# Masked attention layer on one core: where the late tiles are turned, which engine forms two block sums, and when one bias row is subtracted

## The chip, the cores and the metric

The kernel runs on one core of a Trainium2 chip. The metric is the device time of one execution in microseconds (us). The engines are named as the profile names them: PE is TensorE, DVE is VectorE, ACT is ScalarE, POOL is GpSimd, SP is SyncE; PEld is PE's weight load.

## What is computed

The input x has 2708 rows of 1024 numbers, adj is a 2708 x 2708 matrix of zeros and ones with about four ones in a row. In float32:

```python
h = relu(layernorm(x))
q, k, v = h @ Wq.T + bq, h @ Wk.T + bk, h @ Wv.T + bv
z = (q @ k.T) / 32 * adj
z = where(z == 0, -10000, z)
out = x + relu(softmax(z, axis=1) @ v)
```

## The kernel before

**The algebra.** Because a row of adj has few ones, nothing of size 2708 x 2708 is multiplied. Three products of matrices are left: M = Wq.T Wk, made once; "q" rows h M; and the output rows u Wv.T, where u is the weighted sum of those rows of h that the ones of adj name. A score is the dot product of one q row with one row of h, and both scores and weighted sums are made row by row on DVE, from rows of h that POOL gathers out of DRAM (`gather`, L611).

**Tiles and units.** Rows are sorted by their number of ones and cut into tiles of 128. The main loop (from L1244) goes over *units*. A unit is a pair of tiles that is multiplied by a 1024 x 1024 matrix with seven block products instead of eight, as Strassen and Winograd do it. Units 0 to 9 are "q" pairs, units 10 to 19 are "o" (output) pairs, and one single tile comes last. The attention of all tiles is a generator (`attention`), of which `advance(us)` takes as many steps as fit into the time given; a step of a score or of a sum counts as 1.3.

**One unit on PE.** `multiply` runs the blocks in the order s2, a12, s4, s3, then a11 and s1 *of the next unit* (`opened`), then its own a22. A block is four matmul instructions of 128x512, 8 records in the trace. Between blocks it calls `after(i)`, where everything else is issued: after(0) and after(1) stand ahead of s2, after(2) behind s2, after(3) behind a12, after(4) behind s4, after(5) behind s3 and after(6) at the end. DVE's order is that of the program text (`manual_schedule`); the orders of ACT, POOL, SP and PE in the late units are a scheduler's.

**Turning a pair.** The tiles must stand with columns in partitions. `blocks` (L712 on) returns `upper`, called in after(0) of the unit before, and `lower`, called in after(2). There are two ways:
- *by PE*: eight 128x128 transposes of a tile into PSUM (L416), which ACT copies out for a11, a12 and a22 (L719), while DVE makes s1 and s3 out of PSUM (L723);
- *faced*: ACT rewrites the finished u row into v with its columns rearranged (L962) and stores it (`u_dram`, L964); SP loads it back in four pieces of 32 rows (`by_quarters`, L701); DVE transposes 32x32 squares (`faces`, L706), one instruction for each of the two halves of a tile, and then forms s1 (L723) and s3 (L743).

The sums s2 = s1 - a11 and s4 = a12 - s2 (L723) are made by DVE or by POOL, as the caller of `blocks` says: by POOL for units 1 and 2 and for every pair with a faced tile, otherwise by DVE.

**Which tiles are faced** is decided at the end of `sums` (L957 to L968). A tile that is done more than about two units before its own unit is faced, except the last single one; a tile done later is `held` in SBUF when its unit is near, or else stored unturned by SP (L968) and loaded back in one piece (L1226).

**The end of a block product.** In an o unit, c12 (after block s4) is a DVE sum (L1144) and a ReLU on ACT (L1145); c22 (after s3) is a copy out of PSUM on ACT, `taken` (L1094), a DVE sum (L1140) and a ReLU (L1141). PE's block a22 writes the bank that `taken` has read, so it waits for it. In q units the same places are L1113 and L1110.

**The bias row.** `bp_sb` holds the row that starts the PSUM banks of a pair (`banks_for`, L761). It is q's bias until unit 9's banks are filled; at after(4) of unit 8 SP loads b_v into it (L1327) and DVE subtracts one half from the other (L1328).

**Pace.** `share` (L1252) is what `advance` gets at each of a unit's seven calls: 20/7 in q units, 19/7 in o units, less 0.75/7 for each faced tile of the next pair.

Of the kernel before, what the change touches and what calls it, by code (L numbers as in the profile page):

```python
# [65 lines left out]
def tile_preln_masked_attention(  # L66
# [12 lines left out]
    nc = tc.nc  # L79
# [97 lines left out]
    t = 0  # L177
    while t < NT:
# [4 lines left out]
        t = e  # L183
# [28 lines left out]
    def row_tile(name):  # L212
        return work.tile([P, D], FT, tag="row", name=name, bufs=ROWS)
# [401 lines left out]
    rows_of = {}  # L615
    FIRST = EARLY // 2
# [92 lines left out]
    def is_faced(xt):  # L709
        return any(xt is y for y in faced)  # L710
# [57 lines left out]
    ops_of = {0: blocks(*rows_of.pop(0))}  # L768
# [88 lines left out]
    def fill():  # L857
        while wanted and free:
            t, s = wanted.pop(0)
            g = free.pop(0)  # L860
            if s == K[t]:
                half = slice(HOSTS.index(t) * HP, (HOSTS.index(t) + 1) * HP)
                nc.gpsimd.dma_start(g[:HP], v_dram[half, :])
            else:
                with tc.issue_after(first_q[0].ins) if first_q else nullcontext():
                    gathered.append(gather(g, h_dram[:, :], t, s, P, skip=True))
            g_of[t].append(g)

    def chained(step):

        with tc.issue_after(chain[-1].ins):
            chain.append(step())
# [64 lines left out]
    def sums(t):  # L937
        u, coef, m = us.pop(t)
        for s in range(0 if t in EMPTY else 1, K[t]):
            fill()  # L940
            chained(lambda: nc.vector.scalar_tensor_tensor(  # L941
                u, g_of[t][s], coef[:, s:s + 1], u, op0=ALU.mult, op1=ALU.add))
            free.append(g_of[t][s])
            yield 1.3
        fill()
        if t in HOSTS:
            chained(lambda: nc.vector.scalar_tensor_tensor(
                u[:HP], g_of[t][K[t]][:HP], m[:HP, 3:4], u[:HP], op0=ALU.mult, op1=ALU.add))
            free.append(g_of[t][K[t]])
            yield 1.3  # L950
            fill()
        g_of.pop(t)
        if t == SECOND:
            nc.sync.dma_start(v_dram, u)
            whole_second.append(True)
            return
        unit = next((n for n, pair in enumerate(units) if pair[0] == "o" and t in pair[1:]), len(units))  # L957
        if now < [unit - 2, 2] and t != alone:
            faced_tiles.add(t)
        if t in faced_tiles:  # L960
            v = row_tile(f"v_{t}")
            nc.scalar.copy(v.rearrange("p (a c r) -> p c a r", a=QUADS, r=QP),  # L962
                           u.rearrange("p (c a r) -> p c a r", a=QUADS, r=QP))
            nc.scalar.dma_start(u_dram[t * P:(t + 1) * P, :], v)  # L964
        elif near(t):
            held[t] = u
        else:
            nc.sync.dma_start(u_dram[t * P:(t + 1) * P, :], u)  # L968
        done.add(t)
# [37 lines left out]
    faced_tiles, whole_second = set(), []  # L1007
# [4 lines left out]
    spent, now = [0.0], [0, 0]  # L1012
# [193 lines left out]
    q_pairs = [(t, t + 1) for t in range(0, BARE, 2)]  # L1206
    o_pairs = [(order[i], order[i + 1]) for i in range(0, FULL - 1, 2)]
    alone = order[-1]
# [21 lines left out]
    last_q = len(q_pairs) - 1  # L1230
# [13 lines left out]
    for n, unit in enumerate(units):  # L1244
        kind, ta, tb = unit
        now[:] = n, 0
        if n == FIRST:
            ordered.close()
            ordered.enter_context(tc.manual_schedule(engines={mybir.EngineType.DVE}))
            nc.sync.dma_start(bp_dram, bp_sb[0:1, :])  # L1250
        turn = n in (0, FIRST - 1)
        share = (20.0 if kind == "q" else 19.0) / 7  # L1252
        nxt = units[n + 1] if n + 1 < len(units) else None
        if nxt is not None and nxt[0] == "o":
            share -= 0.75 / 7 * len(set(nxt[1:]) & faced_tiles)
        results = (q_results if kind == "q" else o_results)(ta, tb)

        def after(i):
            now[1] = i
            if (n, i) in steps_ahead:  # L1260
                follow(steps_ahead[n, i])
            if (n, i) == (2, 5):
                owe(8)
                owe(9)
                rows_of[FIRST] = load_rows(units[FIRST])
                owe(10)
                owe(6)
                owe(7)
                rows_of[FIRST + 1] = load_rows(units[FIRST + 1])
                pooled.close()  # L1270
            if (n, i) in ((FIRST, 1), (FIRST, 5)):
                ts_of_wv(i // 2, i // 2 + 2)
            if (n, i) == (FIRST, 5):
                next(stream)
            if (n, i) == (FIRST, 6):
                chain.append(behind[-1])
                next(stream)
                nc.vector.tensor_tensor(bad, bad, total, op=ALU.not_equal)
            if (n, i) == (FIRST + 1, 6):
                marked(EARLY, NT)  # L1280
            if (n, i) == (FIRST + 2, 4):
                nc.vector.tensor_scalar(msq, msq, MLIMIT, None, op0=ALU.is_gt)
            if n > FIRST + 1 or n == FIRST + 1 and i > 1:
                advance(share)
            if nxt is not None:

                if i == (3 if n == 0 else 4 if turn else 0):
                    ops_of[n + 1] = blocks(*rows_of[n + 1], nc.gpsimd if n + 1 < FIRST - 1 or any(
                        is_faced(xt) for xt in rows_of[n + 1]) else None)
                    with tc.issue_after(products[-1].ins) if n + 1 == FIRST else nullcontext():  # L1290
                        ops_of[n + 1][1]()
                if i == (4 if n == 0 else 5 if turn else 2):
                    ops_of[n + 1][2]()
                    rows_of.pop(n + 1)
                    if n == last_q - 1:
                        all_rows()
                if i == 3:
                    banks_of[n + 1] = banks_for(bp_sb)
                if i == 6 and n + 2 < FIRST:
                    natural_rows(n + 2)  # L1300
                if i == (2 if n in (FIRST, last_q) else 4) and n + 2 > FIRST and n + 2 < len(units) and n + 2 not in rows_of:
                    while units[n + 2][0] == "o" and not done.issuperset(units[n + 2][1:]):
                        advance(1.0)
                    rows_of[n + 2] = load_rows(units[n + 2])
            if (n, i) in steps_at:
                follow(steps_at[n, i])
            if (n, i) == (3, 4):
                searched()
            if (n, i) == (3, 5):
                for s in range(8, HIGH):  # L1310
                    for c in range(0, D, D // 4):
                        clear = nc.gpsimd.memset(slots[s][:, c:c + D // 4], 0.0)
                        tc.add_manual_dep(clear.ins, counted_at[-1].ins.name,
                                          mybir.DependencyInfo(mybir.DependencyClass.Sync, mybir.DependencyReason.DATA),
                                          reason="not beside the counts")
            if i == 3 and units[n - 1][0] == "o" and NT - 2 in units[n - 1][1:]:
                tail(NT - 1)
            if nxt is None and i == 1:
                while alone not in done:
                    advance(1.0)  # L1320
                r, = load_rows(("o", alone))
                single["turned"] = turned(r, "alone")
            if nxt is None and i == 3:
                single["banks"] = banks_for(bp_sb)
            if n == last_q - 1 and i == 4:

                nc.sync.dma_start(bp_sb, bv.to_broadcast([P, D]))  # L1327
                nc.vector.tensor_sub(bp_sb[:, NB:], bp_sb[:, NB:], bp_sb[:, :NB])  # L1328

            for k, at in enumerate(((0, 0), (0, 1), (0, 3), (0, 4), (0, 5), (0, 5), (1, 2))):  # L1330
                if (n - last_q, i) == at:
                    place, src = ((M[:, 0, 0], of_wv(0, 0)), (T[:, 0], tv_dram[0]), (T[:, 1], tv_dram[1]),
                                  (M[:, 1, 0], of_wv(1, 0)), (M[:, 1, 1], of_wv(1, 1)), (T[:, 2], tv_dram[2]),
                                  (T[:, 3], tv_dram[3]))[k]
                    nc.sync.dma_start(place, src)

        multiply(n, results, after)
# [54 lines left out]
    with tc.If(some > 0):  # L1392
# [19 lines left out]
        with tc.tile_pool(name="big", bufs=1, side="right") as big, tc.tile_pool(  # L1412
# [34 lines left out]
            with tc.For_i(0, NT) as i:  # L1447
# [9 lines left out]
                q = gen.tile([P, D + 1], FT, tag="q", name="g_q")  # L1457
# [111 lines left out]
```

## Time and profile before

| what | us |
|---|---|
| time, median of 3 runs | 660.05 (660.03 to 660.17) |
| time of the profiled execution | 655.3 |
| its span, first to last instruction | 653.6 |
| PE, DVE, ACT, POOL busy in it | 629.9, 530.7, 283.5, 391.0 |
| mean granted PE clock | 0.987 of full speed |

The profile comes from one execution, which was 4.75 us shorter than the median of the runs; 1.7 us of its time lie outside the span. A unit has seven blocks of about 3.43 us, so a q or o unit takes PE 24 us when it waits for nothing, and the tiles turned by PE come on top. A busy PE says little here, since a matmul at a lower clock is busy for longer: look for gaps before matmuls, and for blocks that last longer than 3.60 us in the timeline.

### The profile page before, as it was taken

How to read it: one execution, taken by the hardware profiler on the slowest of the kernel's cores; microseconds unless marked ns; L12 is line 12 of the kernel's file. 1: busy time of each engine (PE TensorE's matmuls, PEld its weight loads, DVE VectorE, ACT ScalarE, POOL GpSimd, SP SyncE). 2: the span in 40 equal slices, each digit the busy share in tenths (PEclk: the TensorE clock that was granted, in tenths of full speed). 3: DMA queues.
4: the chain of work that ended last, by engine and by line, in shares of the span. 5: the costliest groups of instructions: out<-in, count | busy, mean ns of one | idle time of the engine just before them, and what ended most of it. 6: DMA issues, size and time to landing. Idle time of an engine off the chain costs nothing.

```text
span 653.6 us, 6202 instructions
## 1 busy us (share of the span) xinstructions
PE 629.9 (96%) x1603; PEld 314.7 (48%) x1603; DVE 530.7 (81%) x1014; ACT 283.5 (43%) x419; POOL 391.0 (60%) x401
## 2 busy tenths in 40 slices
PE   9999999999999999999999899999798999979994
PEld 5777776444444544444444344444343444434441
DVE  5999699988996648897858969999878998898621
ACT  3549974947775723533412044343332332323300
POOL 2649951966766657645422816768876788772421
PEclk9999999999999999999999999999988999989998
DMA  8998998596898879984899998999999989983551
GB/s 339 407 358 305 363 336 311 179 370 252 326 367 315 303 250 409 346 294 145 319 286 335 306 405 196 342 325 322 330 301 327 310 209 348 288 238 81 132 168 58
DMA packets 68257, 189.55 MB, mean 290 GB/s; under 512 B 10695, under 2 KB 19223, under 8 KB 67320
## 3 DMA queue, kind: packets, MB, share of 16 engines
q1 hardware_dynamic: 36714, 88.05, 38.7%
q0 software_dynamic: 25136, 78.41, 38.2%
q10 hardware_dynamic: 6366, 22.63, 8.9%
q8 instruction: 15, 0.25, 0.2%
q14 instruction: 26, 0.21, 0.1%
HBM read 152.99 MB, written 45.98 MB: 304 GB/s over the span
## 4 chain that ended last, share of the span: by engine, by line
PE 60%; DMA 16%; DVE 12%; issue 6%; POOL 3%; ACT 1%; SPq 0%; POOLq 0%; DVEq 0%; ACTq 0%
PE ps L1029 24%; PE psy L1029 17%; DMA g<-h_dram,tab 8%; PE ps_y L477 6%; DMA or<-u_dram 5%; DVE u L941 5%; PE ps_x L477 4%; PE ps_z L477 4%; DVE junk L881 4%; PE pt L416 3%; DMA y<-in_x_dram,tab 2%; POOL g L611 2%; DVE a L706 1%; DMA bp_sb<-in_bv_dram 1%; DVE s L723 1%
## 5 line engine op out<-in xcount | busy, mean ns | idle before, releaser
L1029 PE MATMUL psy<-wlow,s 128*128 128x512 f32 x320 | 144.2, 593 | 1.9 <-issue 1.3
L1029 PE MATMUL ps<-M,a 128*128 128x512 f32 x320 | 144.0, 593 | 0.0
L611 POOL DMA_INDIRECT g<-h_dram,tab x87 | 107.2, 1233 | 50.9 <-issue 17.1
L881 DVE SCALAR_TENSOR_TENSOR junk<-g,pq 128x1024 uint8<-128x1024 f32 x86 | 111.0, 1290 | 13.1 <-DMA g<-h_dram,tab 10.6
L941 DVE SCALAR_TENSOR_TENSOR u<-g,coef,u 128x1024 f32<-128x1024 f32 x67 | 91.7, 1369 | 5.0 <-ACT u L930 3.6
L1029 PEld LDWEIGHTS psy<-wlow,s 128*128 128x128 f32 x320 | 59.7, 190 | 74.0 <-issue 71.3
L1029 PEld LDWEIGHTS ps<-M,a 128*128 128x128 f32 x320 | 59.9, 190 | 71.3 <-issue 70.1
L1029 PE MATMUL psy<-wlow,a 128*128 128x512 f32 x160 | 78.8, 639 | 10.7 <-ACT taken L1094 9.3
L390 DVE FIND_INDEX8 at<-ones,adj 128x8 uint32<-128x685 f32 (+1 forms) x88 | 74.5, 865 | 0.0
L1029 PE MATMUL ps<-wlow,s 128*128 128x512 f32 x160 | 72.0, 593 | 0.9 <-DVE s L723 0.9
L1029 PE MATMUL ps<-M,s 128*128 128x512 f32 x160 | 71.9, 592 | 0.0
L1029 PEld LDWEIGHTS psy<-wlow,a 128*128 128x128 f32 x160 | 32.2, 205 | 54.7 <-issue 38.3
L369 ACT ACTIVATE sized<-adj 128x2708 uint8<-128x2708 f32 (+1 forms) x22 | 54.3, 2467 | 7.5 <-DMA adj<-in_adj_dram 6.2
L299 POOL TENSOR_TENSOR hsum<-hsum,x 128x256 f32<-128x256 f32 (+1 forms) x56 | 38.6, 735 | 25.7 <-DVE wlow L445 21.6
L1128 POOL DMA_INDIRECT y<-in_x_dram,tab x19 | 32.6, 1716 | 28.1 <-ACT y L1145 16.0
L1029 PEld LDWEIGHTS ps<-wlow,s 128*128 128x128 f32 x160 | 30.3, 190 | 39.5 <-issue 36.6
L1029 PEld LDWEIGHTS ps<-M,s 128*128 128x128 f32 x160 | 30.3, 190 | 38.1 <-issue 37.8
L826 POOL DMA_INDIRECT out_dram<-y,tab x21 | 29.5, 1405 | 28.8 <-DMA y<-in_x_dram,tab 17.1
L611 POOL DMA_INDIRECT M<-h_dram,tab x17 | 22.4, 1318 | 18.0 <-DVE u L941 14.2
L277 ACT ACTIVATE x<-x,r 128x1024 f32<-128x1024 f32 (+1 forms) x22 | 25.9, 1234 | 7.4 <-POOL r L267 7.4
L627 POOL DMA_INDIRECT tab_dram<-tab,pos_i x22 | 22.4, 1018 | 11.1 <-DVE pos_i L690 5.6
L890 ACT ACTIVATE w<-zall 128x4 f32<-128x4 f32 (+6 forms) x20 | 4.1, 207 | 56.1 <-DVE junk L881 56.0
(252 smaller groups left out, 899.7 us busy)
## 6 DMA issues: line engine op xcount, KB each, us to landing
adj<-in_adj_dram SPq DMA_DIRECT2D x21, 1354.0 KB, 10.4
x<-in_x_dram SPq DMA_DIRECT2D x21, 512.0 KB, 7.8
h_dram<-x ACTq DMA_DIRECT2D x21, 512.0 KB, 8.8
u_dram<-v ACTq DMA_DIRECT2D x16, 512.0 KB, 7.7
or<-u_dram SPq DMA_DIRECT2D x64, 128.0 KB, 9.8
q_late<-q SPq DMA_DIRECT2D x12, 512.0 KB, 7.6
pq<-q_late SPq DMA_DIRECT2D x12, 512.0 KB, 7.8
g<-in_wv_dram SPq DMA_DIRECT2D x16, 256.0 KB, 7.4
```

The costliest lines, as they stand in the source:

```text
L277: nc.scalar.activation(xs[i][:n], xs[i][:n], AF.Relu, bias=r[:n, 4, i:i + 1], scale=r[:n, 3, i:i + 1])
L299: small.append(nc.gpsimd.tensor_add(hsum[:n, cols], hsum[:n, cols], xt[:n, cols]))
L369: nc.scalar.activation(sized[:n], a[:n, :, :PW], AF.Abs, accum_out=total[:n, t:t + 1])
L390: nc.vector.max_index(at[:n, k - first_k, g, :], ones[:n, 0:8], a[:n, g, :])
L477: mm = nc.tensor.matmul(bank, a_tile(o + H * a[0], a[1], i), b(o), start=first and o == 0, stop=(o == H - 1), skip_group_check=True)
L611: return nc.gpsimd.indirect_dma_start(out=dst, out_offset=None, in_=src, in_offset=off, bounds_check=N - 1, oob_is_err=False)
L627: put = nc.gpsimd.indirect_dma_start(out=tab_dram[lo >= EARLY][:, :], out_offset=bass.IndirectOffsetOnAxis(ap=pos_i[:n, t:t + 1], axis=0), ...
L826: to = nc.gpsimd.indirect_dma_start(out=out, out_offset=bass.IndirectOffsetOnAxis(ap=ptab.bitcast(U32)[:n, t, SLOTS:SLOTS + 1], axis=0), i ...
L881: chained(lambda: nc.vector.scalar_tensor_tensor(junk, g_of[t][s], 1.0, tq[t], op0=ALU.mult, op1=ALU.mult, accum_out=zall[:, t, s:s + 1]))
L941: chained(lambda: nc.vector.scalar_tensor_tensor(u, g_of[t][s], coef[:, s:s + 1], u, op0=ALU.mult, op1=ALU.add))
L1029: mm = nc.tensor.matmul(bank, a[:, c, :], b[:, c, :], start=False, stop=(c == 3), skip_group_check=True)
L1128: return nc.gpsimd.indirect_dma_start(out=y[:n], out_offset=None, in_=x, in_offset=off, compute_op=ALU.add)
```

## The change

Five edits:

1. A tile is faced only if its unit is one of 10 to 14, the first five output pairs. Before, 16 tiles were faced (64 loads of quarters), in all pairs but the last; in the changed kernel 10 are, and PE turns ten tiles of the output pairs instead of four.
2. POOL takes s2 and s4 of the next pair for every next unit but unit 3. In the order of instructions POOL has 36 of these sums instead of 22; the 14 that come over from DVE belong to units 4 to 9 and 19.
3. The subtraction in the bias row moves from after(4) of unit 8 to after(1) of unit 9. The load stays where it was.
4. The pace in o units is 19.8/7 instead of 19/7.
5. It is lowered by 1.3/7 instead of 0.75/7 for each faced tile of the next pair.

```diff
@@ sums
-        if now < [unit - 2, 2] and t != alone:
+        if now < [unit - 2, 2] and unit <= len(q_pairs) + 4:
             faced_tiles.add(t)
@@ main loop
-        share = (20.0 if kind == "q" else 19.0) / 7
+        share = (20.0 if kind == "q" else 19.8) / 7
...
-            share -= 0.75 / 7 * len(set(nxt[1:]) & faced_tiles)
+            share -= 1.3 / 7 * len(set(nxt[1:]) & faced_tiles)
@@ after(i)
-                    ops_of[n + 1] = blocks(*rows_of[n + 1], nc.gpsimd if n + 1 < FIRST - 1 or any(
-                        is_faced(xt) for xt in rows_of[n + 1]) else None)
+                    ops_of[n + 1] = blocks(*rows_of[n + 1], nc.gpsimd if n + 1 != FIRST - 1 else None)
...
             if n == last_q - 1 and i == 4:
 
                 nc.sync.dma_start(bp_sb, bv.to_broadcast([P, D]))
+            if (n, i) == (last_q, 1):
                 nc.vector.tensor_sub(bp_sb[:, NB:], bp_sb[:, NB:], bp_sb[:, :NB])
```

`FIRST` is 4, `last_q` is 9, `len(q_pairs)` is 10.

## Prediction

> **What bounds the kernel now.** The page comes first, then the list of waits for PE. PE is busy nearly always, so only its gaps and its slow blocks can be won.
>
> ```profile
> span 653.6 us, 6202 instructions
> PE 629.9 (96%) x1603; PEld 314.7 (48%) x1603; DVE 530.7 (81%) x1014; ACT 283.5 (43%) x419; POOL 391.0 (60%) x401
> ```
> ```profile
> PE psy L1029 <- ACT taken L1094: 9.3, 3, 3.6
> PE psy L1029 <- DVE q L1110: 1.5, 2, 1.3
> PE psy L1029 <- issue: 1.3, 1, 1.3
> PE ps_y L512 <- POOL hsum L122: 1.2, 1, 1.2
> PE ps L1029 <- DVE s L723: 0.9, 1, 0.9
> PE psy L1029 <- ACT u L1073: 0.6, 1, 0.6
> ```
>
> The 1.2 us are at the start and stay. The other gaps, 9.3 + 1.5 + 1.3 + 0.9 + 0.6 = 13.6 us, all lie late. PE's timeline shows a block of ordinary length, then the three after the long gaps (start, length, what, gap before):
>
> ```profile
> 465.59 3.60 PE L1029 MATMUL ps<-wlow,s 128*128 128x512 f32 x8
> 472.76 6.75 PE L1029 MATMUL psy<-wlow,a 128*128 128x512 f32 x8 [3.57 <-ACT taken L1094]
> 502.42 5.40 PE L1029 MATMUL psy<-wlow,a 128*128 128x512 f32 x8 [2.31 <-ACT taken L1094]
> 581.62 5.24 PE L1029 MATMUL psy<-wlow,a 128*128 128x512 f32 x8 [3.38 <-ACT taken L1094]
> ```
>
> These are blocks a22 of units 13, 14 and 17. They last 3.15 + 1.80 + 1.64 = 6.6 us too long, because PE's clock has dropped; the table by stretches (PE, PEld, DVE, ACT, POOL busy, then granted clock, DMA share, GB/s) gives 0.77 around the first. So PE loses 13.6 + 6.6 = **20.2 us**, which is all there is to win.
>
> ```profile
> 465.00:480.00 15.00, 11.43 (x20) 4.64 (x19) 13.23 (x17) 4.59 (x8) 12.64 (x9) 0.77 1.05 310
> 585.00:600.00 15.00, 15.00 (x48) 7.52 (x47) 13.16 (x25) 6.45 (x12) 3.78 (x3) 1.00 0.56 140
> 342.80:610.40 267.60, 254.00 (x597) 112.00 (x596) 240.59 (x364) 86.98 (x145) 173.25 (x120) 0.97 0.92 285
> 210.00:342.80 132.80, 132.80 (x372) 63.17 (x371) 99.54 (x176) 49.17 (x85) 72.97 (x73) 1.00 0.85 296
> ```
>
> Why is `taken` late, a copy on an engine that is a third busy? The timeline around the first gap:
>
> ```profile
> 455.29 3.60 PE L1029 MATMUL ps<-M,s 128*128 128x512 f32 x8
> 469.71 0.68 DVE L1144 TENSOR_TENSOR u<-ps,u 128x512 f32<-128x512 f32 x1
> 470.42 0.63 ACT L1145 ACTIVATE y<-u 128x512 f32<-128x512 f32 x1 [3.53 <-DVE u L1144]
> 472.14 0.57 ACT L1094 COPY taken<-psy 128x512 f32<-128x512 f32 x1
> ```
>
> Block s4 ends at 458.89, but DVE gets to its sum at 469.71: **DVE lags PE by 10.8 us**. ACT waits 3.53 us for that sum with `taken` behind it. The third row of the table closes the account: from 342.8 to 610.4 PE would need 254.0 - 6.6 = 247.4 us, while DVE is busy 240.6 and idle 27.0. DVE, one stream in program order, cannot wait 27 us and keep PE's pace: 240.6 + 27.0 - 247.4 = 20.2, just what PE loses. The last row, q units, is different: DVE is busy 99.5 of 132.8 us, and PE has no gap.
>
> **The change, part by part.**
>
> *Bias row.* DVE stands still for the load:
>
> ```profile
> 334.82 7.31 DMA bp_sb<-in_bv_dram
> 342.83 0.68 DVE q L1110
> ```
> ```profile
> DVE bp_sb L1328 <- DMA bp_sb<-in_bv_dram: 5.9, 1, 5.9
> ```
>
> The sum moves behind about ten attention steps, when the load has landed. DVE enters the late stretch **5.9 us earlier**. SP loses nothing: the load is issued where it was. ACT's copies of the row into unit 10's banks stand at after(3) of unit 9, two blocks or 6.9 us behind the new place of the sum, so DVE may lag that much before they wait. In the new order of SP the store of v_dram comes ahead of two weight loads; it waits for DVE sums that now come before them, so I cost it at nothing (if DVE were late again, those loads would be).
>
> *Fewer faced tiles.* Six tiles, so 12 DVE transposes fewer and 48 PE transposes more. Rows: DVE groups (busy, mean ns), ACT's rewriting of u, and one tile's eight PE transposes in the chain.
>
> ```profile
> L706 DVE STREAM_TRANSPOSE a<-or 128x512 f32<-128x512 f32 x25 | 16.6, 692 | 4.5 <-DMA or<-u_dram 3.7 <-PE psy L1029 0.9
> L723 DVE TENSOR_TENSOR s<-a,s 128x512 f32<-128x512 f32 x16 | 11.1, 693 | 0.8
> ```
> ```profile
> 586.86 0.87 PE pt L416 x8
> ```
>
> PE pays 6 x 0.87 = **5.2 us**, all on its path. DVE saves 12 x 0.69 = 8.3 us. ACT copies turned blocks but rewrites fewer u; at 87.0 us busy of 267.6 it hides either. Four finished tiles are now stored by SP, which waits there for DVE with loads queued behind: that is rival C. Would the transposes cost clock? In 585-600, with two tiles turned, it is 1.00, and I add nothing. The Trainium skill ("TensorE: Matmul & The Clock Gate", "Part 4: PE-mode transpose") says that transposes do not count as PE activity in the usual way. By that rule each of six more turnings could bring a slow block like that at 502 us, 1.80, and the sum would be 10.8 us higher; the row of 585-600 speaks against it.
>
> *s2 and s4 on POOL.* Twelve of the 14 belong to q units. DVE saves 0.69 us each, but two engines disturb each other:
>
> ```profile
> 483.00 1.22 DVE L881 SCALAR_TENSOR_TENSOR junk<-g,pq 128x1024 uint8<-128x1024 f32 x1
> 493.20 2.29 DVE L881 SCALAR_TENSOR_TENSOR junk<-g,pq 128x1024 uint8<-128x1024 f32 x1
> 494.49 2.12 POOL L723 TENSOR_TENSOR s<-a,s 128x512 f32<-128x512 f32 x1
> L723 POOL TENSOR_TENSOR s<-a,s 128x512 f32<-128x512 f32 x11 | 20.1, 1829 | 0.8
> L723 POOL TENSOR_TENSOR s<-s,a 128x512 f32<-128x512 f32 x11 | 15.5, 1409 | 9.9 <-DVE s L723 9.7
> ```
>
> A DVE step of 1.22 us becomes 2.29 beside a POOL sum: each moved sum saves 0.69 and costs up to 1.07. By these rows this edit alone slows DVE. The Trainium skill ("SBUF — State Buffer", "Who interferes with whom") states an exclusive lock: a DVE instruction with two SBUF inputs and a GpSimd instruction that reads SBUF block each other for a whole instruction. By that rule a sum could hold DVE for all its 2.12 us instead of 1.07; unit 19's pair would cost DVE 2.1 us more, too little to move the forecast; the 1.07 of the trace decides. In q units 33 us of idle DVE time hide six times 2 x (1.07 - 0.69) = 4.6 us. In the late stretch only unit 19's pair is new: -1.4 + 2.1 us. On POOL a pair takes 1.83 + 1.41 = 3.24 us ahead of queued gathers. One place is tight, the rows of unit 7 (issue on POOL, then PE's two turnings):
>
> ```profile
> 256.92 1.93 POOL L613 DMA_INDIRECT qr<-h_dram,tab  x1 [0.30 <-issue]
> 259.16 0.97 POOL L613 DMA_INDIRECT qr<-h_dram,tab  x1 [0.30 <-issue]
> ```
> ```profile
> qr<-h_dram,tab POOLq DMA_INDIRECT x12, 7.7
> ```
> ```profile
> 267.77 0.87 PE pt L416 x8
> 272.08 0.87 PE pt L416 x8
> ```
>
> The new order puts unit 6's pair of sums ahead of both gathers: 256.92 + 3.24 + 7.7 = 267.9 for a turning at 267.77. Between 0 and 1.5 us; I take **0.5**. For the other units the turning comes 10 us or more after the gather.
>
> *Pace.* Against faced pairs DVE gets 17.2 instead of 17.5 of attention a unit, otherwise 19.8 instead of 19.0 or less. The sum of steps is the same; it shifts to units where PE has 1.74 us more to do. No price of its own.
>
> **The account after the change.** From 342.8 on PE needs 247.4 + 5.2 = 252.6 us. DVE needs 240.6 - 8.3 - 1.4 + 2.1 = 233.0, and 260.0 if it waits 27.0 as before; it begins 5.9 earlier, so 254.1. The deficit of 20.2 us shrinks to 1.5, which its permitted lag swallows: a22 comes three blocks behind s4, so 10.3 less DVE's 0.68 and ACT's 0.63 and 0.57, **8.4 us** at most. On the mean PE is then the bound. But waits do not come evenly, and a22 blocks are released by DVE in every unit. I leave one stall of the size of that at 502 us, 2.31 + 1.80 = 4.1 us (bounds: 0, or two of the three). Sum: -20.2 + 5.2 + 0.5 + 4.1 = **-10.4 us**. From the profiled execution's 655.3 that is 644.9; from the median 660.05, which I take as base, **649.6**.
>
> **Rivals.**
>
> *A. No stall is left.* -20.2 + 5.2 = -15.0: **645.0**. For it: the deficit of 1.5 us. Against it: 1.5 us is a mean over ten units, and one unit that gets several waits goes past the permitted lag.
>
> *B. DVE's relief is half eaten by waits for gathers.* The DMA share is 1.05 around 470, so starting earlier can mean waiting longer. The stalls of units 13 and 17 stay, 3.57 + 3.15 + 3.38 + 1.64 = 11.7: -20.2 + 5.2 + 0.5 + 11.7 = -2.8, **657.3**.
>
> *C. Slower: DMA sets DVE's pace entirely, and PE now waits for the rows itself.* Landing times in 450-510, and SP's wait at unit 13:
>
> ```profile
> or<-u_dram SPq DMA_DIRECT2D x18, 128.0 KB, 12.8
> ```
> ```profile
> SPq L1148 <- ACT y L1145: 11.8, 1, 11.8
> ```
>
> In the new SP order the load of unit 15's second row stands behind the tail's store (L1148), which waits for unit 13's ReLU. From the end of s4 it lands after lag + 0.68 + 0.63 + 12.8; PE wants it after five blocks of 3.43 and one turning, 18.0 (12.8 is that of quarters, the nearest row). So PE stalls from a lag of 3.9 us on; at 10.8 it waits 6.9, of which it has spent 6.7 in the stall of unit 13 anyway. If the lag stays, the three stalls stay (15.9) and 0.2 is added: -20.2 + 15.9 + 0.2 + 5.2 + 0.5 = +1.6, **661.7**. It decides if DVE's idle time in the late stretch grows from 27 to over 41 us (233.0 + 41.4 - 5.9 - 252.6 = 15.9). Against it: DVE waits for gathers only 10.6 us in all:
>
> ```profile
> L881 DVE SCALAR_TENSOR_TENSOR junk<-g,pq 128x1024 uint8<-128x1024 f32 x86 | 111.0, 1290 | 13.1 <-DMA g<-h_dram,tab 10.6 <-DMA pq<-q_dram,tab 0.8
> ```
>
> **How the numbers follow.** Forecast 0.40, A 0.20, B 0.17, C 0.16, and 0.07 for a result between B and C within 0.2% (1.3 us, about what can be told from no change). Faster: 0.40 + 0.20 + 0.17 = 0.77; same 0.07; slower 0.16. The range runs from 643.5 (A, less its rounding and the small gaps between matmuls) to 659.5 (beyond B), leaving out C and the edge of "same".
>
> **What would show it.** Right: no wait for DVE ahead of L1328; PE's waits for `taken` under 4 us with the clock near 1.00 after 400 us; 48 more transposes on PE at 0.87 us for eight; DVE's lag at L1144 under 8 us in units 12 to 18; no new gap before q-unit blocks above 1.5 us. Wrong: PE waiting ahead of L416 for `or` (C); DVE's waits for `g` well over 10.6 us (B, C); or DVE steps stretched for longer than 1.07 us a sum in q units, so that gaps appear there.

## The result and the profile after

| | before | changed |
|---|---|---|
| median of 12 runs each, us | 660.83 (658.78 to 664.28) | 654.94 (652.02 to 658.57) |
| ratio, 95% interval | | 0.9912 (0.9891 to 0.9932) |
| profiled execution and its span, us | 655.3, 653.6 | 654.2, 652.5 |

The change saves 5.9 us, 0.9%. The forecast was a saving of 10.4, so the direction was right and the size was not: 4.5 us are missing.

The page of the changed kernel gives the span and the busy times:

```profile
span 652.5 us, 6269 instructions
PE 631.6 (97%) x1651; PEld 318.5 (49%) x1651; DVE 525.0 (80%) x988; ACT 281.6 (43%) x423; POOL 403.1 (62%) x415
```

PE has the 48 transposes more (1651 records against 1603) and DVE 26 instructions less. At 0.69 us each, 26 instructions are 17.9 us of busy time; DVE lost only 5.7. (By the prediction's stretch of up to 1.07 us for each of the 14 moved sums it would have lost 2.9.) The list of waits for PE, in which each row gives the waiting tile and line, what it waited for, and then total, number and longest in us:

```profile
PE ps L1029 <- DVE s L723: 4.5, 1, 4.5
PE psy L1029 <- ACT psy L1042: 1.9, 1, 1.9
PE pt L416 <- DMA qr<-h_dram,tab: 1.6, 1, 1.6
PE ps_y L512 <- POOL hsum L122: 1.2, 1, 1.2
PE ps L1029 <- DMA M<-in_wv_dram: 0.9, 1, 0.9
PE psy L1029 <- DMA wlow<-tv_dram: 0.8, 1, 0.8
PE psy L1029 <- ACT u L1073: 0.8, 1, 0.8
PE ps L1029 <- ACT ps L761: 0.5, 1, 0.5
```

Every wait for `taken` is gone. In their place stands one wait of 4.5 us for s, of a kind that was 0.9 before. PE's timeline shows where, and that two weight loads come late just ahead of it:

```profile
383.77 3.67 PE L1029 MATMUL ps<-M,s 128*128 128x512 f32 x8 [0.91 <-DMA M<-in_wv_dram]
...
388.27 3.67 PE L1029 MATMUL psy<-wlow,s 128*128 128x512 f32 x8 [0.83 <-DMA wlow<-tv_dram]
...
399.88 6.25 PE L1029 MATMUL ps<-wlow,s 128*128 128x512 f32 x8 [4.50 <-DVE s L723]
```

The last block lasts 6.25 us instead of 3.60, so the stall costs 4.50 + 2.65 = 7.15 us. It lies where unit 10 passes into unit 11. DVE's list of waits says why s1 was late, and DVE's timeline when:

```profile
DVE junk L881 <- DMA pq<-q_late: 14.4, 1, 14.4
```
```profile
395.19 1.23 DVE L881 SCALAR_TENSOR_TENSOR junk<-g,pq 128x1024 uint8<-128x1024 f32 x1 [14.44 <-DMA pq<-q_late]
```

DVE stands from 380.75 to 395.19 and waits for the q rows of one tile (pq); s1 of the next pair stands behind two scores in its order. In the kernel before, the wait ahead of the same score was 4.19 us, and for gathered rows:

```profile
386.14 1.22 DVE L881 SCALAR_TENSOR_TENSOR junk<-g,pq 128x1024 uint8<-128x1024 f32 x1 [4.19 <-DMA g<-h_dram,tab]
```

**Unit by unit.** One row of PE's timeline for each unit is enough to see where time goes: the start of block s1, `ps<-wlow,s`. The first and the last row used, of the kernel before and of the changed one (units 4 and 19):

```profile
209.05 3.60 PE L1029 MATMUL ps<-wlow,s 128*128 128x512 f32 x8
...
605.61 3.60 PE L1029 MATMUL ps<-wlow,s 128*128 128x512 f32 x8
```
```profile
214.16 3.17 PE L1029 MATMUL ps<-wlow,s 128*128 128x512 f32 x7
...
604.75 3.60 PE L1029 MATMUL ps<-wlow,s 128*128 128x512 f32 x8
```

From the first to the last it is 396.6 us before and 390.6 after: 6.0 us less, close to the 5.9 of the medians; single profiles scatter by more than that difference, so the closeness is partly luck. Of the whole profiled executions this shows only 1.1, because the kernel before was lucky ahead of unit 4: its unit 3 took 25.8 us, that of the changed kernel 29.7 (there are the waits of 1.9 and 1.6 us for `psy` and `qr`, at 193 and 206 us). The change is not the cause: the first experiment below runs the kernel before unchanged up to unit 8, and its unit 3 took 32.3. That the profiled 655.3 us of before lie 5.5 under the median of its twelve runs fits with this. The difference stands ahead of all edits and is left out below.

The steps from s1 of one unit to s1 of the next, in us (24.0 is PE's own time with no tile turned, 24.9 with one, 25.8 with two):

| unit | 9 | 10 | 11 | 12 | 13 | 14 | 15 | 16 | 17 | 18 |
|---|---|---|---|---|---|---|---|---|---|---|
| before | 24.5 | 28.3 | 25.0 | 24.0 | 24.0 | 30.9 | 28.3 | 24.9 | 24.9 | 31.0 |
| changed | 24.0 | 30.9 | 26.7 | 24.0 | 24.0 | 25.8 | 25.8 | 25.9 | 26.9 | 25.8 |

Units 14, 15 and 18 hold the three stalls for `taken`; there 12.8 us are won although each pays for turned tiles. Units 10 and 11 lose 4.3, units 16 and 17 lose 3.0 (1.7 of it turning).

### The profile page after: what moved, and what is told of

It is laid out like the page before. It is cut to its first block, busy times and chain, and to the rows that moved or that the text cites. A ratio compares the mean times of both kernels' runs of the same rounds, so it can differ in the third digit from the quotient of the medians.

```text
span 652.5 us, 6269 instructions
## 1 busy us (share of the span) xinstructions
PE 631.6 (97%) x1651; PEld 318.5 (49%) x1651; DVE 525.0 (80%) x988; ACT 281.6 (43%) x423; POOL 403.1 (62%) x415
## 4 chain that ended last, share of the span: by engine, by line
PE 58%; DMA 13%; DVE 13%; issue 8%; POOL 4%; ACT 2%; another core or an unknown queue 0%; POOLq 0%; DVEq 0%; SPq 0%; ACTq 0%
PE ps L1029 23%; PE psy L1029 16%; DMA g<-h_dram,tab 7%; PE ps_y L477 6%; DVE u L941 5%; DVE junk L881 4%; PE ps_x L477 4%; PE ps_z L477 4%; PE pt L416 3%; DMA y<-in_x_dram,tab 2%; POOL g L611 2%; DMA h_dram<-x 2%; DMA qr<-h_dram,tab 1%; DMA M<-in_wv_dram 1%; ACT sized L369 1%
## 5 line engine op out<-in xcount | busy, mean ns | idle before, releaser
L611 POOL DMA_INDIRECT g<-h_dram,tab x87 | 105.1, 1207 | 44.9 <-issue 18.0
L881 DVE SCALAR_TENSOR_TENSOR junk<-g,pq 128x1024 uint8<-128x1024 f32 x86 | 110.5, 1285 | 22.5 <-DMA pq<-q_late 14.4
L941 DVE SCALAR_TENSOR_TENSOR u<-g,coef,u 128x1024 f32<-128x1024 f32 x67 | 94.3, 1408 | 3.9 <-ACT u L930 2.4
L1029 PE MATMUL ps<-wlow,s 128*128 128x512 f32 x160 | 74.7, 611 | 4.5 <-DVE s L723 4.5
L1029 PE MATMUL psy<-wlow,a 128*128 128x512 f32 x160 | 71.9, 592 | 0.0
L299 POOL TENSOR_TENSOR hsum<-hsum,x 128x256 f32<-128x256 f32 (+1 forms) x56 | 38.6, 730 | 27.4 <-DVE wlow L445 23.5
L1029 PEld LDWEIGHTS psy<-wlow,a 128*128 128x128 f32 x160 | 30.4, 190 | 38.3 <-issue 37.8
L1128 POOL DMA_INDIRECT y<-in_x_dram,tab x19 | 33.1, 1740 | 17.7 <-ACT y L1145 8.0
L723 POOL TENSOR_TENSOR s<-s,a 128x512 f32<-128x512 f32 x18 | 24.2, 1346 | 30.9 <-DVE s L723 30.7
L930 ACT ACTIVATE u<-g,coef 128x1024 f32<-128x1024 f32 x15 | 17.2, 1150 | 37.6 <-DVE coef L929 33.5
L723 POOL TENSOR_TENSOR s<-a,s 128x512 f32<-128x512 f32 x18 | 29.6, 1646 | 1.2
L627 POOL DMA_INDIRECT tab_dram<-tab,pos_i x22 | 22.2, 1008 | 11.8 <-DVE pos_i L690 6.3
```

Source lines behind the costliest of these rows:

```text
L299: small.append(nc.gpsimd.tensor_add(hsum[:n, cols], hsum[:n, cols], xt[:n, cols]))
L611: return nc.gpsimd.indirect_dma_start(out=dst, out_offset=None, in_=src, in_offset=off, bounds_check=N - 1, oob_is_err=False)
L627: put = nc.gpsimd.indirect_dma_start(out=tab_dram[lo >= EARLY][:, :], out_offset=bass.IndirectOffsetOnAxis(ap=pos_i[:n, t:t + 1], axis=0), ...
L723: step = (eng or nc.vector).tensor_tensor(ops[name], a, b, op=op)
L881: chained(lambda: nc.vector.scalar_tensor_tensor(junk, g_of[t][s], 1.0, tq[t], op0=ALU.mult, op1=ALU.mult, accum_out=zall[:, t, s:s + 1]))
L941: chained(lambda: nc.vector.scalar_tensor_tensor(u, g_of[t][s], coef[:, s:s + 1], u, op0=ALU.mult, op1=ALU.add))
```

## The experiments

All were timed against the kernel before on the same chip, four at a time; its median was 661.3, 657.2 and 661.4 us in the three sets (e1 to e4, e5 to e8, e9 to e12). So times that an expectation names are read as differences, and the gain here is (ratio - 1) x 660.8 us with its 95% interval. "9 to 18" is the sum of the ten units above in the profile. "DVE's two waits" are those for the bias row at after(4) of unit 8 and for the first score that waits in unit 10; the first does not exist where the subtraction is moved.

| kernel | gain, us | 9 to 18 | 10 and 11 | DVE's two waits |
|---|---|---|---|---|
| before | | 265.8 | 53.3 | 5.9 + 4.2 |
| changed | -5.8 (-7.2 to -4.5) | 259.8 | 57.6 | 14.4 |
| e1 bias row alone | +1.7 (-0.3 to +3.6) | 269.0 | 56.8 | 12.5 |
| e2 changed, no bias edit | -6.5 (-8.9 to -4.1) | 259.0 | 51.6 | 6.3 + 5.6 |
| e3 changed, no POOL edit | -10.0 (-13.1 to -6.9) | 254.3 | 52.0 | 10.9 |
| e4 changed, q stores on ACT | -7.3 (-10.0 to -4.7) | 258.7 | 53.2 | 11.8 |
| e5 changed, POOL not in q units | -7.5 (-9.6 to -5.3) | 258.5 | 55.6 | 13.4 |
| e6 facing and pace alone | -9.8 (-11.6 to -8.2) | 254.9 | 51.8 | 5.9 + 5.8 |
| e7 changed, old facing | -1.8 (-3.0 to -0.5) | 263.3 | 59.4 | 16.0 |
| e8 changed, old pace | -1.9 (-3.5 to -0.1) | 263.0 | 60.1 | 15.0 |
| e9 changed, M ahead of quarters | -5.0 (-6.7 to -3.3) | 261.5 | 57.8 | 14.0 |
| e10 as e6, late sums on DVE | -10.6 (-13.2 to -8.1) | 258.3 | 51.5 | 5.1 + 7.2 |
| e11 facing alone | -4.8 (-6.8 to -2.8) | 261.2 | 52.0 | 8.6 + 4.6 |
| e12 pace alone | -5.4 (-7.1 to -3.6) | 257.1 | 54.0 | 5.5 + 6.9 |

One profile is one execution: e3 and e5 have the same instructions up to unit 13, and their units 10 and 11 differ by 3.6 us. Differences of that size in a profile alone decide nothing below.

### What the bias row is worth: e1 and e2

e1 is the kernel before with this edit only; e2 is the changed kernel without it.

```diff
                 nc.sync.dma_start(bp_sb, bv.to_broadcast([P, D]))
+            if (n, i) == (last_q, 1):
                 nc.vector.tensor_sub(bp_sb[:, NB:], bp_sb[:, NB:], bp_sb[:, :NB])
```

> The kernel before with edit 3 alone (the subtraction of the bias row in after(1) of unit 9). My theory (the gain is DVE's relief, and part of it is lost to a load of q rows that comes late because the weight loads bunch up behind the quarters on SP): DVE's 5.9 us ahead of the subtraction go, but the order on SP becomes that of the changed kernel, so the wait for pq in unit 10 grows from under 5 to about 14 us; the stalls for taken stay. 658 to 662 us against 660.8, that is between -3 and +1. Rival 1 (the bias row alone carries the gain): 655, -6, with the stalls for taken gone. Rival 2 (the long wait for pq was an accident of one profile): the wait for pq is under 6 us in this profile and the time is 655 to 657.

> The changed kernel without edit 3: the subtraction stays in after(4) of unit 8, the other four edits are in. My theory: DVE waits 5.9 us for the bias row as before, but one quarter-row order on SP is as before (one M load ahead of the quarters), the wait for pq stays under 6 us, and 12 fewer transposes on DVE leave stalls for taken of 4 to 8 us: 651 to 656 us, -10 to -5. Rival 1 (the bias row alone carries the gain): no gain is left, and the 5.2 us of turning on PE make it 660 to 666. Rival 2 (accident): the wait for pq is the same with and without edit 3.

Measured: e1 +1.7 us, a little above the -3 to +1 of my theory, its interval holding zero; e2 -6.5 against -5.8 for the changed kernel, and without the stalls for `taken` that I expected there. Facing and pace with it (e3, -10.0) and without it (e6, -9.8) are alike too. Three pairs of kernels say the same: the bias row is worth nothing that can be told from zero. Rival 1 falls. The rows of e1 show a stall that it gained beside the three that it kept:

```profile
PE psy L1029 <- ACT taken L1094: 8.8, 3, 3.7
PE ps L1029 <- DVE s L723: 6.8, 1, 6.8
```
```profile
DVE junk L881 <- DMA pq<-q_late: 12.5, 1, 12.5
```

Rival 2 (an accident of one profile) falls as well. In the eight kernels with the edit the wait in unit 10 is 10.9 to 16.0 us, in the six without it 4.2 to 7.2. The last column points to the mechanism: without the edit DVE's two waits add up to 10.1 to 13.2 us, 11.9 in the mean; with it the one wait is 13.5 in the mean. **The wait was not removed but moved**, from a place where PE had work in hand to one where PE soon needed s1. Counted from block s1 of unit 9, DVE goes on behind the wait in unit 10 after 46.3 to 49.5 us without the edit and after 46.6 to 51.9 with it, so no earlier.

### Why pq lands late: e4 and e9

Edit 3 also changed SP's order in a way that the prediction did not list. A load of M for the output units, which left ahead of the eight quarters of unit 11's rows, now leaves behind them: 22.2 us after block s1 of unit 9 starts, where it was 14.4. The kernel before, then the changed one:

```profile
354.17 0.33 SPq L1335 DMA_DIRECT2D M<-in_wv_dram  x1
```
```profile
367.11 2.64 SPq L1335 DMA_DIRECT2D M<-in_wv_dram  x2
```

e1 has the new order and e2 the old one, so it comes with edit 3. Two experiments act on the order. e4 issues the two stores of unit 9's q rows on ACT, so that pq is not queued behind them on SP. e9 restores one piece of SP's old order: a load of M goes ahead of all but one of the quarters of unit 11's rows.

```diff
-            (nc.scalar if t < 4 else nc.sync).dma_start(dst, q)
+            (nc.scalar if t < 4 or t >= BARE - 2 else nc.sync).dma_start(dst, q)
```
```diff
-                if i == (2 if n in (FIRST, last_q) else 4) and n + 2 > FIRST and n + 2 < len(units) and n + 2 not in rows_of:
+                if i == (2 if n == FIRST else 5 if n == last_q else 4) and n + 2 > FIRST and n + 2 < len(units) and n + 2 not in rows_of:
```

> The changed kernel, and the two stores of unit 9's q rows are issued on ACT instead of SP, so that the load of pq for tile 17 behind them on SP no longer waits for ACT's copy. My theory: the load goes out 6 to 8 us earlier, the wait for pq in unit 10 falls from 14.4 us to under 8, PE's wait for s in unit 10 (4.5 us and a slow block of 2.65 us more) goes: 648 to 651 us, 4 to 7 less than the changed kernel's 654.9. Rival 2 (accident of one profile): 654 to 656, as the changed kernel, with the wait for pq under 6 us in both. Rival 5 (the DMA engines are full there, so the load takes longer by what it starts earlier): the wait for pq stays over 11 us and the time within 1.5 us of the changed kernel.

> The changed kernel, but the rows of unit 11 are loaded from after(5) of unit 9 instead of after(2), so that on SP a load of M and all but one of the eight quarters change places, as in the kernel before. Theory S (the order on SP makes pq late): DVE's wait for pq in unit 10 falls from 14.4 to under 8 us, PE's unit 10 from 30.9 to under 28 us, and the time is 9 to 11 us under that of the kernel before. Theory D (the DMA engines are full from 340 to 395 us whatever the order, so what DVE gains ahead of the stretch it waits for in it): the wait for pq stays over 11 us, and the gain on the kernel before is 4 to 7.5 us, as with the changed kernel.

Measured: -7.3 and -5.0, neither to be told from -5.8. In the changed kernel, then in e4, SP issues the load at these times:

```profile
379.32 0.44 SPq L851 DMA_DIRECT2D pq<-q_late  x1
```
```profile
373.30 0.33 SPq L851 DMA_DIRECT2D pq<-q_late  x1
```

In e4 the load leaves 6.0 us earlier, but DVE goes on only 4.2 us earlier, at 391.0 instead of 395.2 (1.6 us of both is a lead that e4 has since unit 4). From issue to use it takes 17.7 us where it took 15.9: 1.8 us of what it gains in leaving is lost on the way. Its wait for pq, 11.8 us, is not shorter than the 10.9 of e3, which keeps the changed kernel's order. So my theory for e4 failed; rival 5 held, narrowly (over 11 us, and 1.5 us from the changed kernel's gain). In e9 theory S failed and theory D held: the wait for pq is as long as ever, and M now stalls PE, its last load leaving only at 373.17, behind seven quarters:

```profile
387.84 6.75 PE L1029 MATMUL ps<-M,s 128*128 128x512 f32 x8 [6.41 <-DMA M<-in_wv_dram]
```
```profile
DVE junk L881 <- DMA pq<-q_late: 14.0, 1, 14.0
```

So the order on SP, which I suspected after seeing the result, changes which load is late; neither new order brought a gain that can be told from the changed kernel's. The table by stretches (busy PE, PEld, DVE, ACT, POOL, then clock, DMA share, GB/s) shows the likely reason, for the kernel before and for the changed one:

```profile
340.00:395.00 55.00, 51.28 (x118) 21.90 (x118) 44.98 (x75) 14.55 (x25) 22.39 (x17) 1.00 0.96 332
```
```profile
340.00:395.00 55.00, 53.26 (x124) 23.02 (x122) 38.65 (x59) 13.45 (x22) 20.24 (x16) 1.00 1.03 345
```

For 55 us the DMA engines are full or nearly so, before and after: seven loads for the weights of the output units, quarters, gathers and stores meet here. By this reading an engine that comes earlier to a stretch in which DMA is the bound waits longer in it by about as much. The sums of the waits and both experiments fit; no run took traffic out of the stretch, so that DMA is the bound here is argued and not shown.

### Sums on POOL: e3, e5 and e10

e3 takes edit 2 back. POOL then has 14 sums instead of 36, since the old rule gives it the pairs with a faced tile. e5 takes POOL out of units 4 to 9 only (24 sums). e10 is edits 1, 4 and 5 with no sum of an output pair on POOL (4 sums). Below is only the last argument of `blocks`.

```diff
-nc.gpsimd if n + 1 != FIRST - 1 else None
+nc.gpsimd if n + 1 < FIRST - 1 or any(is_faced(xt) for xt in rows_of[n + 1]) else None   # e3
+nc.gpsimd if n + 1 < FIRST - 1 or n + 1 > last_q else None                               # e5
+nc.gpsimd if n + 1 < FIRST - 1 else None                                                 # e10
```

> The changed kernel without edit 2: DVE keeps s2 and s4 of units 4 to 9 and 19. My theory: the 12 sums of the q units lie in DVE's idle time and cost nothing either way, unit 19's pair under 2 us: 653 to 657 us, within 2 us of the changed kernel's 654.9. Rival 3 (the sums on POOL stretch DVE's steps and hold up gathers, so that edit 2 costs what the change fell short of): 650, 4 to 5 us less than the changed kernel. Rival 4 (edit 2 is what frees DVE): 660 or more.

> The changed kernel, but DVE makes s2 and s4 for units 4 to 9; POOL keeps those of units 1 and 2 and of all output pairs, 24 sums in all. The kernel without edit 2 (14 sums on POOL) was 4 us faster than the changed kernel (36). This run tells where that lies. Theory L (in the last five units, 15 to 19, where each sum on POOL stretches DVE's steps by up to 1.07 us and PE is released late): 653 to 656 us, as the changed kernel; PE's unit times after 500 us as there. Theory Q (in units 4 to 9: the sums hold up gathers and loads, and DVE meets unit 10 with more to wait for): 649 to 652, with DVE's wait for pq in unit 10 under 12 us.

> Edits 1, 4 and 5 alone, and POOL makes s2 and s4 for units 1 and 2 only: DVE makes all those of the output pairs, so POOL has 4 sums (14 with edits 1, 4, 5; 36 in the changed kernel). In the runs so far the last 22 sums on POOL saved DVE 22 x 0.69 = 15.2 us and stretched its score and sum steps by 13.3. Theory (a sum on POOL costs DVE about what it saves, and holds POOL's gathers besides): 8 to 12 us less than the kernel before, within 2 us of the kernel with edits 1, 4 and 5; no POOL sum beside a late DVE step, so their mean is 1.22 and 1.29 us. Rival (the faced pairs need POOL, since DVE has 20 transposes there): 3 to 7 us less than the kernel before, with PE's units 10 to 13 longer than 27.1, 24.7, 24.1 and 25.1 us by 1 each.

Measured: -10.0, -7.5 and -10.6. My theory for e3 (nothing either way) failed and rival 3 held: without edit 2 the kernel is 4.2 us faster, though the two intervals overlap by 0.3. The pair e6 and e2, the same comparison without the bias edit, gives 3.3 (-9.8 against -6.5). e5 lies between the two, nearer to theory L, but its interval touches what theory Q asked for, so the times do not divide the loss between early and late sums. The units show a part that is late: unit 17 takes 26.9 to 28.1 us in the five kernels with new facing, new pace and POOL's late sums (the changed one, e2, e4, e5, e9), and 25.8, PE's bound, in the four without sums beyond unit 14 (e3, e6, e10, e11); e8, with those sums and the old pace, has 25.8 too, so it takes both. For e10 the theory held and the rival fell: units 10 to 13 take 27.4, 24.1, 24.0 and 24.0 us. Its profile has a wait of 6.9 us for gathers in unit 14, so that the ten units look worse than the timed runs.

DVE's groups show the cost. The changed kernel, then e10:

```profile
L881 DVE SCALAR_TENSOR_TENSOR junk<-g,pq 128x1024 uint8<-128x1024 f32 x86 | 110.5, 1285 | 22.5 <-DMA pq<-q_late 14.4 <-DMA g<-h_dram,tab 4.6 <-issue 1.9
L941 DVE SCALAR_TENSOR_TENSOR u<-g,coef,u 128x1024 f32<-128x1024 f32 x67 | 94.3, 1408 | 3.9 <-ACT u L930 2.4
...
L723 POOL TENSOR_TENSOR s<-a,s 128x512 f32<-128x512 f32 x18 | 29.6, 1646 | 1.2
L723 POOL TENSOR_TENSOR s<-s,a 128x512 f32<-128x512 f32 x18 | 24.2, 1346 | 30.9 <-DVE s L723 30.7
```
```profile
PE 628.7 (97%) x1651; PEld 317.5 (49%) x1651; DVE 518.1 (80%) x1020; ACT 282.4 (43%) x423; POOL 358.0 (55%) x383
```
```profile
L881 DVE SCALAR_TENSOR_TENSOR junk<-g,pq 128x1024 uint8<-128x1024 f32 x86 | 105.2, 1224 | 22.9 <-DMA g<-h_dram,tab 13.1 <-DMA pq<-q_late 7.2 <-DMA pq<-q_dram,tab 0.9
L941 DVE SCALAR_TENSOR_TENSOR u<-g,coef,u 128x1024 f32<-128x1024 f32 x67 | 85.9, 1282 | 3.9 <-ACT u L930 2.4
```

e10 has 32 more instructions on DVE and is busy 6.9 us less there. So a sum that went to POOL saved DVE 0.69 us and cost it (6.9 + 32 x 0.69) / 32 = 0.91 us: moving it was a loss for the very engine that it was to relieve. (e10 lacks edit 3 too; e3, which differs from the changed kernel in edit 2 alone, has 22 instructions more and is busy 3.5 us less, which gives 0.85.) The Trainium skill ("SBUF — State Buffer", "Who interferes with whom") says that a DVE instruction with two SBUF inputs and a GpSimd instruction that reads SBUF shut each other out; these rows agree, with 0.91 us in the mean for POOL sums of 1.35 to 1.65. Whether the gathers that queue behind POOL's wait for s1 (30.7 us in all, 16.7 in e3) add to the loss was not tried by itself.

### Facing and pace: e6, e7, e8, e11 and e12

e6 is the kernel before with edits 1, 4 and 5; e7 is the changed kernel without 1, e8 without 4 and 5; e11 is edit 1 alone, e12 is 4 and 5 alone. In e7 and e12 15 tiles are faced and not 16, because the new pace moves one past its limit.

```diff
-        if now < [unit - 2, 2] and t != alone:                  # old in e7, e12
+        if now < [unit - 2, 2] and unit <= len(q_pairs) + 4:    # new in e6, e8, e11
...
-        share = (20.0 if kind == "q" else 19.0) / 7             # old in e8, e11
+        share = (20.0 if kind == "q" else 19.8) / 7             # new in e6, e7, e12
...
-            share -= 0.75 / 7 * len(set(nxt[1:]) & faced_tiles)
+            share -= 1.3 / 7 * len(set(nxt[1:]) & faced_tiles)
```

> The kernel before with edits 1, 4 and 5 alone: 10 tiles faced instead of 16, and the new pace; the bias row and the choice of POOL are as before (which gives POOL 14 sums, since POOL takes them for a pair with a faced tile). Theory (facing fewer tiles is the whole gain, the bias row is worth nothing, and the sums on POOL cost 4 us): 649 to 652 us, -12 to -9. Rival (the bias row's 5.9 us are needed once the sums are on DVE): 654 to 658. If PE's unit times after 500 us are 25.8 us each, PE alone bounds that part.

> The changed kernel without edit 1: all tiles that are done early are faced again; the bias row, POOL's sums and the new pace stay. Theory (facing is the whole gain): the stalls for taken are back, 659 to 663 us, against 660.8 for the kernel before. Rival (pace and bias row together remove the stalls): 654 or less, since PE then also saves 5.2 us of turning.

> The changed kernel without edits 4 and 5: the pace is 19/7 less 0.75/7 for each faced tile, as before. My theory (pace has no price of its own): 653 to 657 us, within 2 us of the changed kernel's 654.9. Rival (the pace matters: against the units with faced pairs DVE would get more attention and lag again): 658 or more, with waits for taken.

> The kernel before with edit 1 alone. With edits 1, 4 and 5 the gain was 9.8 us, and the changed kernel without edits 4 and 5 gained 1.8. Theory P (the pace has a price only behind the long wait for pq of the bias edit): 8 to 10 us less than the kernel before. Rival (facing and pace each carry part): 3 to 7 less, with one stall for taken of 2 to 4 us around unit 13, where the old pace gives DVE more attention than the new.

> The kernel before with edits 4 and 5 alone: the tiles are faced as before but for one, since the pace moves one past the limit. Theory P (pace without less turning on DVE gives nothing): within 2 us of the kernel before, with the stalls for taken of over 2 us in two units at least. Rival (facing and pace each carry part): 3 to 7 us less than the kernel before.

Measured: -9.8, -1.8, -1.9, -4.8 and -5.4. My theory for e8 (the pace has no price) failed: taking the pace away costs 3.9 us. So did the theory that facing is the whole gain, and theory P for e11 and for e12, where the rival held: facing and pace carry about half each, and they add up (-4.8 - 5.4 = -10.2, with both -9.8). Of e7 the expected size (-2 to +2) was right but the ground was not, as facing is not the whole gain.

They do not remove the same stalls. The units of these kernels:

| unit | 9 | 10 | 11 | 12 | 13 | 14 | 15 | 16 | 17 | 18 |
|---|---|---|---|---|---|---|---|---|---|---|
| e11 facing alone | 28.8 | 27.0 | 25.0 | 24.0 | 24.0 | 29.1 | 25.8 | 25.8 | 25.8 | 25.8 |
| e12 pace alone | 24.1 | 28.2 | 25.8 | 24.0 | 24.1 | 24.8 | 27.4 | 24.9 | 27.5 | 26.2 |
| e6 both | 24.5 | 27.1 | 24.7 | 24.1 | 25.1 | 26.3 | 25.8 | 25.8 | 25.8 | 25.8 |

Facing brings units 15 to 18 to PE's bound, since no pair after 14 needs DVE's transposes, but it leaves the stall for a22 of unit 13; the pace takes that one away. The pace also shortens unit 18 from 31.0 to 26.2 us, but unit 15 stays 3.4 us above its 24.0 and unit 17, which turns two tiles here, 1.7 above its 25.8. The same block in e11, then in e12:

```profile
479.34 3.70 PE L1029 MATMUL psy<-wlow,a 128*128 128x512 f32 x8 [3.06 <-ACT taken L1094]
```
```profile
473.81 3.70 PE L1029 MATMUL psy<-wlow,a 128*128 128x512 f32 x8
```

(After this gap of 3.06 us the block takes 3.70 us, hardly longer than usual; after the 2.31 us at 502 us in the kernel before it took 5.40. So the length of a gap alone does not say whether a slow block follows.)

In e12 DVE has 12 score and sum steps to make between c22 of unit 12 and c22 of unit 13, where it had 13 before. Beside POOL's sums two small steps (L924, L929) take 1.3 us longer together; before, four score and sum steps took 4.2 us longer. So DVE comes out of unit 12 later (4.9 us after block s1 of unit 13 starts, 3.0 before) and out of unit 13 earlier (3.5 us after s1 of unit 14 starts, 7.5 before). e8 shows the other side. With the old pace and the bias edit, the long wait for pq is followed by a stall of 6.0 us (6.8 in e1, which has both too), where the changed kernel has 4.5:

```profile
PE ps L1029 <- DVE s L723: 6.0, 1, 6.0
```
```profile
DVE junk L881 <- DMA pq<-q_late: 16.5, 2, 15.0
```

**The best kernels.** e6 and e10 beat both kernels, with gains of 9.8 and 10.6 us whose intervals lie above that of the change; e3, at 10.0, has an interval that just touches it. Among the three none is the best by measurement. e6 is the simplest: three of the five edits. Its page, its two waits, and a late stretch:

```profile
span 643.1 us, 6241 instructions
PE 628.6 (98%) x1651; PEld 317.7 (49%) x1651; DVE 520.8 (81%) x1010; ACT 282.4 (44%) x423; POOL 370.4 (58%) x393
```
```profile
DVE junk L881 <- DMA pq<-q_late: 6.0, 2, 5.8
DVE bp_sb L1328 <- DMA bp_sb<-in_bv_dram: 5.9, 1, 5.9
```
```profile
490.00:595.00 105.00, 105.00 (x293) 49.94 (x292) 94.23 (x142) 35.50 (x64) 63.06 (x46) 1.00 0.81 246
```

From 490 to 595 us PE has no gap. DVE still waits for the bias row as before, and it does no harm.

## Why the prediction was right and wrong

**Right: the bound and its cause.** PE lost time late because DVE lagged. The prediction's account does not prove it, though: DVE's busy and idle time fill the 267.6 us of the stretch in any kernel, and so do PE's need and its loss, so the 20.2 on both sides is one number found twice. The experiments show it: e11 takes turning away from DVE and e12 moves its steps, and each removes stalls. With 12 transposes fewer on DVE, and steps shifted by the pace, all three stalls for `taken` went. From unit 12 to unit 18 DVE's sum L1144 starts 5.0 to 7.4 us after the end of block s4, as forecast under 8. The table by stretches, changed kernel:

```profile
400.00:420.00 20.00, 20.00 (x41) 8.68 (x42) 19.19 (x35) 9.34 (x17) 11.98 (x10) 0.87 0.80 202
465.00:480.00 15.00, 15.00 (x36) 6.65 (x35) 14.24 (x24) 5.09 (x10) 10.56 (x10) 1.00 1.03 387
342.80:610.40 267.60, 260.56 (x660) 118.66 (x659) 237.03 (x360) 86.27 (x151) 170.68 (x124) 0.99 0.91 285
```

At 465 to 480, where the clock was 0.77, it is 1.00. The sign "near 1.00 after 400 us" failed in one place: it is 0.87 from 400 to 420, just behind the stall for s1.

**Right: the price on PE.** One tile's turning, from its first transpose to the next block, is 482.37 - 481.49 = 0.88 us, forecast 0.87; six tiles are 5.2 to 5.3.

```profile
481.49 1.04 PE L416 MATMUL pt<-ident,or 128*128 128x128 f32 x8
482.37 3.60 PE L1029 MATMUL psy<-wlow,s 128*128 128x512 f32 x8
```

The price in clock that the Trainium skill's rule on transposes ("TensorE: Matmul & The Clock Gate", "Part 4: PE-mode transpose") would add does not show: in e6 each of the units 15 to 18 turns two tiles, and from 490 to 595 us, which they fill, the granted clock is 1.00.

**Wrong: "SP loses nothing" and "DVE enters the late stretch 5.9 us earlier".** This is the step that failed. DVE did come earlier: no wait stands ahead of the subtraction. But the account charged DVE the 27.0 us of idle time that it had before, as if waits for DMA kept their length when DVE moves. The end of the wait in unit 10 stayed instead, and e1, e2, e3 and e6 show that the 5.9 us are worth nothing. In the stretch from 342.8 DVE is idle for 30.6 us, not 27.0, and busy for 237.0, not 233.0. Nor did SP lose nothing: the store of v_dram, which the prediction looked at, did no harm, but a load of M moved behind eight quarters, and PE waited 0.9 us for M and 0.8 us for another weight. That the full DMA engines hold the end of the wait is the likely cause, but not shown. The sum allowed one stall of 4.1 us for the whole late stretch; units 10 and 11 alone lost 7.15 + 0.9 + 0.8 = 8.9. Rival B named this mechanism (starting earlier can mean waiting longer, DMA share above 1), but it placed the stalls at `taken`, and its sign, longer waits for `g`, did not come: they fell from 10.6 to 4.6 us, and the wait was for pq.

**Wrong: s2 and s4 on POOL (0.5 us).** The twelve sums in q units cost PE nothing there, as said: units 4 to 8 take the same time in both kernels to 0.1 us, so the 0.5 us for unit 7's rows did not come. But without edit 2 the kernel is 3 to 4 us faster. I took the late sums as given, because POOL made them before; with fewer faced tiles, though, the old rule would have handed eight of them back to DVE, and edit 2 kept them on POOL. I had the row (a step of 1.22 us becomes 2.29) and the verdict that the edit by itself slows DVE, and then summed only the units in which the assignment changes against the kernel before.

**Wrong: pace (no price).** It is worth about 4 us here and 5.4 alone. The sum of steps stays, but a stall depends on the one unit that has a step too many, not on the sum.

**Wrong in detail: the permitted lag of 8.4 us.** It holds where ACT runs `taken` behind the ReLU L1145. In unit 11 `taken` stands ahead of it, 6.8 us in ACT's timeline of the changed kernel, and the lags at L1144, 17.9 and 9.6 us in units 10 and 11, bring no wait for `taken`:

```profile
423.38 0.59 ACT L1094 COPY taken<-psy 128x512 f32<-128x512 f32 x1 [2.85 <-PE psy L1029]
430.16 0.63 ACT L1145 ACTIVATE y<-u 128x512 f32<-128x512 f32 x1 [1.76 <-DVE u L1144]
```

**The sum by what was measured.** From unit 4 on, PE's waits in the changed kernel are 4.5 + 0.9 + 0.8 + 0.8 + 0.5 = 7.5 (the list above, without `ps_y` at the start and `psy` and `qr` in unit 3), and the slow block adds 2.65: 10.2 us of loss where 20.2 were, and 4.6 were forecast. -20.2 + 5.2 + 10.2 = -4.8, against -6.0 by the units and -5.9 by the medians; about 1.2 us stand in no row of the list. The error of the forecast is mainly this loss of 5.6 us more than I allowed; the turning and the stalls removed were sized right. That the result still came as near as it did is partly luck. The account credited edit 3, which is worth nothing, and put edit 2 near zero, which costs 3 to 4 us; but it also gave no value to the pace, which is worth about 4.

## What to carry to other kernels

Before you credit an engine with an earlier start, look at what bounds the stretch it starts into: where DMA is full, a wait that is removed can come back at the next load, perhaps at a worse place. Work given to an engine that shares a resource with the one to be relieved must be summed over all that stays there, not only over what is moved, since the rest of the change may have made it needless. And stalls belong to single units: compare the bound engine's time unit by unit, from one marked instruction to the next, and a change of half a per cent becomes a row of numbers that says where to look. Which edit did what is then for timed runs to say, since one profile is one execution.

## What was not expected of the hardware

The DMA share says that the engines are full, and not how much they move. Two stretches of the changed kernel, both full, and the packets in them:

```profile
360.00:370.00 10.00, 10.00 (x25) 4.50 (x24) 9.93 (x8) 0.64 (x2) 8.82 (x7) 1.00 1.09 215
380.00:390.00 10.00, 8.26 (x19) 3.26 (x18) 0.74 (x1) 2.71 (x4) 0.98 (x1) 1.00 1.02 419
```
```profile
DMA packets 1275, 2.15 MB, mean 215 GB/s; under 512 B 142, under 2 KB 1029, under 8 KB 1219
```
```profile
DMA packets 1103, 4.19 MB, mean 419 GB/s; under 512 B 220, under 2 KB 220, under 8 KB 964
```

215 and 419 GB/s. The first has 1275 packets of 1.7 KB in the mean, the second 1103 of 3.8 KB. Ahead of and in the first SP issues the quarters (pieces of 256 numbers), in the second whole rows are on the way. That the pieces make the difference is likely, but it was not tried by itself.
